# A four-layer image network on one core: small matmuls of the second layer and of the norms in quarters of the array, with a smaller unit time in the planner

## The chip, the core and the metric

The kernel runs on one core of a Trainium2 chip. The core has five engines that work side by side, each through its own queue in order: TensorE (PE; its weight loads are listed as PEld), VectorE (DVE), ScalarE (ACT), GpSimd (POOL) and SyncE (SP), which here only issues transfers. ACT and POOL issue transfers too. Instructions of different engines wait for each other by semaphores. The metric is the device time of one execution in microseconds (us), as the median of several runs.

## What is computed

The input x is 4 images of 96 channels and 64 x 64 pixels in f32. Four layers follow, cut here to their shape:

```python
x = x + ss2d(group_norm(x))               # layer 0: layer norm, projection, 3x3 depthwise conv,
                                          #   four selective scans of 192 channels x 16 states
                                          #   over 4096 pixels, layer norm, gate, projection
x = x + deform_conv(group_norm(x))        # layer 1: offsets = conv3x3(x, 27 outputs), then
                                          #   9 taps sampled at these offsets (bilinear), conv
t = tokens(x)
t = t + fourier(ln(t)); t = t + ffn(ln(t))      # layer 2: 96 -> 192, FFT along 4096 tokens and back
t = t + linear_attention(ln(t)); t = t + ffn(ln(t))   # layer 3
```

The offsets' convolution of layer 1 has 27 outputs for each pixel: 9 vertical offsets, 9 horizontal ones and 9 mask values. A layer norm (`ln`) subtracts the mean over the 96 channels of a pixel and divides by the root of the variance.

## The kernel before

The work of an image is cut into 8 chunks of 512 pixels (`CH`), and channels lie on the partitions. The selective scans of layer 0 are cut into 1536 *units*: 4 images x 4 directions x 4 stretches of 1024 pixels x 3 groups x 8 units, and each has 8 channels x 16 states on the 128 partitions. A unit takes: a transfer of the decay exponents (L874), an exponential on ACT (L895, `da`), two matmuls on PE that spread the inflow over the partitions (L901, `db`, two buffers), a product on DVE (L915), the recurrence itself on DVE (L918, `hh`), two instructions on POOL (L925, L927), and a share of the sums over the states on PE (L946, `py`). The sums already use quarters of PE's columns: each matmul writes 32 partitions of one PSUM tile (`py[p0 : p0 + 32]`) with 32 weight columns. L941 adds an earlier direction's result in four such quarters.

All other work is written as Python generators that are laid between the units. Stream `ends` holds layer 0 before the scan for each image and then layers 2 and 3 of each image; stream `middle` holds layer 0 behind the scan and layer 1. An image's later layers can start only when its scans are done, so the last image's stand behind the last unit.

The order of instructions is fixed when the program is built, by a planner. Each step of a generator names its costs in us by engine (`cost(pe=2.6)`), and class `Clock` adds them up by engine. After every unit `unit()` raises `due` by `PACE`. A step is placed if the engines that it uses have room: the planned end of each may be at most a few us (`AHEAD`) after the present, and the step's `ready`, which its earlier steps set, may not lie after the end of its first engine. `pipe()` runs several chains of such steps at once; a chain may take and give back counted tokens (`takes`, `frees`), for instance for a buffer. The chip knows nothing of this clock: it sees one order for each engine and the semaphores.

The functions that the change touches:

- `centred()` (L447) is the first half of a layer norm, called 4 times each for layer 0, the Fourier layer, attention and the two feed-forward layers, 20 in all. For each chunk PE multiplies by a centring matrix (L457, `lnc`), ACT writes the squares (L462 or L465, `lnq`) and copies the centred values. Then PE sums the squares of chunk j over the channels into row j of a tile of 128 rows (L468, `lnv`, with 128 weight columns of which one is not zero). `inv_sqrt_steps()` makes the root's inverse of the whole tile on ACT and DVE, and `spread()` (L483, `lnb`) brings row j back onto all partitions.
- `offsets()` (L1113) is layer 1 up to the offsets. `chunk(j)` adds nine taps into one tile (L1149, `po`, 96 weight columns of which 27 are not zero), ACT adds the bias (L1159, `oc`), PE transposes the pixels (L1165, `pt`) and the offsets (L1170, `pm`), ACT copies both, and SP writes the pixels into a table in DRAM in eight transfers (L1178, `table<-pix`). The nine taps come in three steps of three.
- `behind()` (L968) has a layer norm over 192 channels, with the sums at L1022 (`va`) and two chunks in rows 0 and 1.

```python
nc.tensor.matmul(var, lhsT=self.to_row[C][:C, 7 - j : 135 - j], rhs=sq, ...)   # L468
```

Of the kernel before, what the change touches and what calls it, by code (L numbers as in the profile page):

```python
# [8 lines left out]
F32 = mybir.dt.float32  # L9
# [16 lines left out]
CH = 512  # L26
# [18 lines left out]
def prepare(x, **w):  # L45
# [65 lines left out]
    om = np.concatenate([ow[0::2], ow[1::2], w["L1_conv_mask_w"].reshape(9, C, 9)])  # L111
    a["wom"] = wide(om.transpose(1, 2, 0), 96)
    ob = w["L1_conv_offset_b"]
# [85 lines left out]

PACE = 4.8  # L200

# [59 lines left out]
def pipe(net, chains, width, every=0, **tiles):  # L261
# [5 lines left out]
    while True:  # L267
# [9 lines left out]
        for n, chain in enumerate(active):  # L277
            if chain.new and not net.has_bank():
                continue
            if any(a.done <= chain.done + every for a in active[:n]):  # L280
                continue
            if not all(free[tag] for tag in chain.takes):
                continue
            if clock.has_room(known.get((chain.kind, chain.done), (1.0,) * 4), chain.ready):
                break
        else:
            yield BLOCKED
            continue
# [44 lines left out]
class Net:  # L333
# [3 lines left out]
    def __init__(self, ctx, tc, ins):  # L337
# [4 lines left out]
        self.psum = ctx.enter_context(tc.tile_pool(name="mm", bufs=3, space=PSUM))  # L342
        for name in ("vecs", "ident", "cen96", "grp3"):
            setattr(self, name, self.load(name, self.const))

        self.to_row = {}
        for n in (C, DI):
            t = self.to_row[n] = self.const.tile([128, 135], F32, name=f"to_row{n}")
            nc.vector.memset(t, 0.0)
            nc.vector.memset(t[:, 7:8], 1.0 / n)  # L350
        self.eps = self.const.tile([128, 1], F32, name="eps")
# [95 lines left out]
    def centred(self, x, cen, dst, key, pool, bias=None):  # L447
# [3 lines left out]
        var = self.mm(f"lnv{key}")  # L451
        self.hold(1)

        def chain(j):
            cs = slice(j * CH, (j + 1) * CH)
            pc = self.mm(f"lnc{key}_{j}")
            nc.tensor.matmul(pc, lhsT=cen, rhs=x[:, cs], start=True, stop=True)  # L457
            pc = pc[:C]
            sq = pool.tile([C, CH], F32, name=f"lnq{key}_{j}", tag="lnq", bufs=2)
            d, view = dst(j)  # L460
            if bias is None:
                nc.scalar.activation(sq, pc, AF.Square)  # L462
                nc.scalar.copy(d, view(pc))
            else:
                nc.scalar.activation(sq, pc, AF.Square, bias=bias)  # L465
                nc.scalar.activation(d, view(pc), AF.Identity, bias=bias)
            yield cost(pe=1.1, act=1.2)
            nc.tensor.matmul(  # L468
                var, lhsT=self.to_row[C][:C, 7 - j : 135 - j], rhs=sq, start=(j == 0), stop=(j == NCH - 1)
            )  # L470
            yield cost(pe=1.0)

        yield from pipe(self, (chain(j) for j in range(NCH)), 2)
        self.rstd = pool.tile([128, CH], F32, name=f"lns{key}", tag="lns", bufs=1)
# [35 lines left out]
class Layer0:  # L510
# [95 lines left out]
    def normed_rows(self, b, x, pad, rows, as_rows):  # L606
# [3 lines left out]
        with tc.tile_pool(name=f"l0n{b}", bufs=2) as sm:  # L610
# [21 lines left out]
            def chain(j):  # L632
                pb = net.spread(rs, j, C, f"0_{b}")
                yield cost(pe=1.2, holds=1)
# [333 lines left out]
    def behind(self, b):  # L968
# [6 lines left out]
        with (  # L975
# [4 lines left out]
            for j0 in range(NCH - HB, -1, -HB):  # L980
# [18 lines left out]
                def centred(i):  # L999
# [12 lines left out]
                    for g, (o, c0, n) in enumerate(((ca, 0, 128), (cc, 128, D2))):  # L1012
# [9 lines left out]
                        nc.tensor.matmul(  # L1022
                            var,
                            lhsT=net.to_row[DI][:n, 7 - i : 135 - i],
                            rhs=sq,
                            start=(i == 0 and g == 0),
                            stop=(i == HB - 1 and g == 1),
                        )
# [8 lines left out]
                def gated(i):  # L1037
# [5 lines left out]
                    nc.sync.dma_start(zc, self.z_d[b][128:, cs])  # L1043
                    pb = net.spread(rstd, i, 128, key)
                    yield cost(pe=1.2, holds=1)
# [25 lines left out]
class Layer1:  # L1071
# [41 lines left out]
    def offsets(self, b, om):  # L1113
# [3 lines left out]
        with tc.tile_pool(name=f"l1a{b}", bufs=1, side="right") as pre:  # L1117
# [26 lines left out]
            def chunk(j):  # L1144
                r0 = j * NR
                po = net.mm(f"po{b}_{j}", 96)
                for k in range(9):
                    dy, dx = divmod(k, 3)
                    nc.tensor.matmul(  # L1149
                        po,  # L1150
                        lhsT=wom[:, k, :],
                        rhs=pad[:, r0 + dy : r0 + dy + NR, dx : dx + W],
                        start=(k == 0),
                        stop=(k == 8),
                    )
                    if k in (2, 5):
                        yield cost(pe=2.6, holds=1, takes="oc" if k == 5 else "")
                oc = pre.tile([27, CH], F32, name=f"oc{b}_{j}", tag="oc")
                nc.scalar.activation(oc, po[:27], AF.Identity, bias=net.vec(V_OMB, 27))  # L1159
                yield cost(pe=2.6, act=0.7, new=True, takes="pix")  # L1160

# [7 lines left out]
                for q in range(4):  # L1169
                    nc.tensor.transpose(pm[:, q, :], oc[:, 128 * q : 128 * q + 128], net.ident[:27, :27])  # L1170
                nc.scalar.copy(om[:, 4 * j : 4 * j + 4, :], pm)
# [292 lines left out]
def normed(net, t, tl, key, pool):  # L1464
# [6 lines left out]
    def chain(j):  # L1471
        cs = slice(j * CH, (j + 1) * CH)
        pb = net.spread(rs, j, C, key)
        yield cost(pe=1.2, holds=1)
        net.nc.vector.tensor_mul(tl[:C, cs], tl[:C, cs], pb)  # L1475
        yield cost(dve=0.7)
# [248 lines left out]
```

## Time and profile before

| | us |
|---|---|
| median of 5 runs | 9117.53 (9101.12 to 9141.04) |
| profiled execution | 9100.43 |
| its span, first to last instruction | 9098.3 |
| first and last start of a scan recurrence (L918) | 369.6 and 7983.1 |
| busy PE, DVE, POOL, ACT | 6723.8 (74%), 6975.9 (77%), 6367.4 (70%), 4183.9 (46%) |
| mean granted clock of TensorE | 0.822 |
| L1149, the taps: busy, 576 records | 266.3 |
| L468, the sums of squares: busy, 320 records | 173.2 |

The page of a profile lists for each line its busy time, the mean of one instruction in ns, the idle time of its engine just before it and what ended that idle time. The chain of waits goes back from the last instruction, at each step to what released it. A matmul of f32 data stands as two records. The trace is of one execution; the profiled one lies a little below the lowest of the five timed ones.

### The profile page before, as it was taken

What the parts mean: (1) busy time and instruction counts of PE and PEld (TensorE: products, weight loads), DVE (VectorE), ACT (ScalarE), POOL (GpSimd) and SP (SyncE); (2) the same over time, 40 slices, a digit from 0 to 9 for tenths busy, and PEclk for the clock granted to TensorE, in tenths of its full rate; (3) what the DMA queues carried; (4) which work ended last, traced back from release to release, by engine and by line L of the source; (5) the groups of instructions that cost most, each with busy time, mean ns of one, the idle gap of its engine ahead of it and who ended that gap; (6) DMA issues with size and microseconds to landing.
All of it is one profiled execution on the core that took longest, in us unless ns stands there. A gap on an engine that the chain in (4) does not pass through costs nothing.

```text
span 9098.3 us, 93017 instructions
## 1 busy us (share of the span) xinstructions
PE 6723.8 (74%) x31832; PEld 3064.7 (34%) x31832; DVE 6975.9 (77%) x4932; ACT 4183.9 (46%) x5798; POOL 6367.4 (70%) x4755
## 2 busy tenths in 40 slices
PE   6565966697766679776778877788777768885487
PEld 2111311132222234211245642244543425433273
DVE  0367877887898888878898989889899988836614
ACT  3564667565554435555533335533344344431123
POOL 0476678766889998787799977766799966627701
PEclk8676978798878789788889888788888878886698
DMA  1466777777877887787788786677777777824410
GB/s 50 126 181 173 184 193 215 199 186 175 211 209 211 214 210 207 199 212 199 206 208 228 208 196 173 170 190 186 210 200 198 197 165 192 196 57 138 133 58 12
DMA packets 775821, 1609.05 MB, mean 177 GB/s; under 512 B 247665, under 2 KB 338829, under 8 KB 773238
## 3 DMA queue, kind: packets, MB, share of 16 engines
q10 hardware_dynamic: 244224, 843.17, 36.9%
q1 hardware_dynamic: 457398, 533.38, 21.8%
q0 software_dynamic: 73728, 226.57, 9.4%
q8 instruction: 253, 4.15, 0.2%
q14 instruction: 218, 1.79, 0.1%
HBM read 1346.50 MB, written 256.29 MB: 176 GB/s over the span
## 4 chain that ended last, share of the span: by engine, by line
PE 32%; DVE 21%; POOL 16%; DMA 14%; issue 9%; ACT 5%; SPq 1%; ACTq 0%; DVEq 0%; POOLq 0%
DVE hh L918 9%; POOL hh L927 7%; DVE db L915 5%; POOL g L1251 5%; PE pc L662 4%; PE py L946 4%; PE f L1371 3%; PE db L901 3%; PE ps L1277 2%; PE po L1149 2%; DMA du<-du 2%; DVE g L1260 2%; PE pd L1293 2%; DMA g<-table,idx 2%; DMA da<-de 1%
## 5 line engine op out<-in xcount | busy, mean ns | idle before, releaser
L927 POOL TENSOR_TENSOR hh<-hh,bc 128x1024 f32<-128x1024 f32 x1536 | 3670.5, 2391 | 350.4 <-DVE hh L918 233.7
L918 DVE TENSOR_TENSOR_SCAN hh<-da,st,db 128x1024 f32<-128x1024 f32 x1152 | 2703.7, 2347 | 220.0 <-PE py L946 71.1
L915 DVE TENSOR_TENSOR db<-db,bc 128x1024 f32<-128x1024 f32 x1536 | 1869.2, 1217 | 409.2 <-PE db L901 399.2
L895 ACT ACTIVATE da<-da,w_al 128x1024 f32<-128x1024 f32 x1536 | 1743.3, 1148 | 729.9 <-DMA da<-de 278.1
L901 PE MATMUL db<-du,rep 96*128 96x512 bf16 x3072 | 1062.2, 433 | 820.6 <-DVE hh L918 756.1
L1251 POOL DMA_INDIRECT g<-table,idx x1152 | 1339.6, 1163 | 400.4 <-issue 227.7
L946 PE MATMUL py<-hh,w_fold 128*32 128x512 f32 x6144 | 1082.6, 731 | 114.0 <-POOL hh L927 90.6
L918 DVE TENSOR_TENSOR_SCAN hh<-da,db 128x1024 f32<-128x1024 f32 x384 | 878.2, 2287 | 61.3 <-PE py L946 9.4
L1277 PE MATMUL ps<-w_ident,g 128*96 128x128 f32 x3744 | 610.9, 323 | 377.1 <-issue 236.1
L901 PEld LDWEIGHTS <-rep 96*128 96x128 bf16 x3072 | 275.3, 104 | 1741.6 <-issue 1167.7
L1260 DVE TENSOR_TENSOR g<-g,wt 128x1152 f32<-128x1152 f32 x384 | 687.2, 1790 | 162.6 <-DMA g<-table,idx 159.9
L1285 ACT COPY st<-ps 96x384 f32<-96x384 f32 x384 | 182.4, 476 | 1249.3 <-PE ps L1277 1088.2
L925 POOL COPY st<-hh 128x1 f32<-128x1 f32 x1152 | 271.5, 236 | 657.7 <-DVE hh L918 623.4
L1277 PEld LDWEIGHTS ps<-w_ident,g 128*96 128x96 f32 x3744 | 499.1, 150 | 611.5 <-issue 354.8
L749 POOL TENSOR_TENSOR w<-w,ex 128x512 f32<-128x512 f32 x192 | 245.9, 1281 | 518.3 <-ACT w L746 512.5
L662 PE MATMUL pc<-pad,wc 96*128 96x512 f32 x1152 | 540.9, 617 | 45.1 <-DMA wc<-wc_d 41.5
L752 DVE SCALAR_TENSOR_TENSOR rl<-pd,lw 128x512 f32<-128x512 f32 x192 | 130.9, 682 | 473.9 <-POOL lw L750 463.3
L771 PE MATMUL pr<-ex,w_ident 128*128 128x512 f32 x384 | 290.1, 847 | 151.6 <-POOL ex L761 75.2
L946 PEld LDWEIGHTS py<-hh,w_fold 128*32 128x32 f32 x6144 | 161.2, 120 | 634.2 <-issue 386.7
L1517 POOL CAST xqf<-fl 96x512 fp8e5<-96x512 f32 x64 | 45.3, 715 | 438.1 <-DVE fl L1475 390.9
L662 PEld LDWEIGHTS pc<-pad,wc 96*128 96x128 f32 x1152 | 222.5, 198 | 329.6 <-issue 314.1
L1293 PE MATMUL pd<-st,wdc 96*128 96x256 f32 x1152 | 311.5, 422 | 1.0 <-ACT zt L688 0.8
(249 smaller groups left out, 9485.3 us busy)
## 6 DMA issues: line engine op xcount, KB each, us to landing
da<-de ACTq DMA_DIRECT2D x1536, 512.0 KB
du<-du SPq DMA_DIRECT2D x512, 192.0 KB
bc<-bcd SPq DMA_DIRECT2D x128, 512.0 KB
du<-du SPq DMA_DIRECT2D x128, 384.0 KB
y<-yb SPq DMA_DIRECT2D x384, 128.0 KB
de<-rl SPq DMA_DIRECT2D x128, 256.0 KB
m<-in_dft SPq DMA_DIRECT2D x128, 256.0 KB
ad<-y ACTq DMA_DIRECT2D x192, 128.0 KB
```

The costliest lines, as they stand in the source:

```text
L662: nc.tensor.matmul(pp, lhsT=wc[:, q, g * 128 : (g + 1) * 128], rhs=pad[:, r0 + dy : r0 + dy + NR, dx : dx + W], start=(q == 0), stop=(q == 8),
L771: nc.tensor.matmul(pr, lhsT=net.ident, rhs=ex, start=True, stop=False)
L895: self.net.nc.scalar.activation(u.da, u.da, AF.Exp, scale=self.al[:, a : a + 1])
L901: self.net.nc.tensor.matmul(db[:, h, :], lhsT=self.rep[:96, u.s % 4, :], rhs=u.du[u.s // 4][:, h * CH : (h + 1) * CH], start=True, stop=True,)
L915: nc.vector.tensor_mul(u.db, u.db, u.bc[:, 0, :])
L918: nc.vector.tensor_tensor_scan(u.along(u.hh), u.along(u.da), u.along(u.db), first, ALU.mult, ALU.add)
L927: self.net.nc.gpsimd.tensor_mul(u.hh, u.hh, u.bc[:, 1, :])
L946: nc.tensor.matmul(py[p0 : p0 + 32], lhsT=self.fold[:, u.i, :], rhs=hc[:, h * CH : (h + 1) * CH], start=u.sums["add"] is None and u.i == 0 ...
L1251: nc.gpsimd.indirect_dma_start(out=g[:, k, :], out_offset=None, in_=self.tables[b % 2], in_offset=bass.IndirectOffsetOnAxis(ap=idx[:, n : ...
L1260: nc.vector.tensor_mul(g4, g4, w4.unsqueeze(2).to_broadcast([128, 12, C]))
L1277: nc.tensor.matmul(pt[:, k, :], lhsT=g[:, k, c * C : (c + 1) * C], rhs=net.ident, is_transpose=True, start=(c == 0), stop=(c == corners - 1),)
L1293: nc.tensor.matmul(po, lhsT=wdc[:, k, :], rhs=st[:, k, :], start=(k == 0), stop=(k == 8))
```

## The change

There are three parts. First, the offsets' convolution uses 32 weight columns instead of 96, and tap k writes partitions 32 (k mod 4) to 32 (k mod 4) + 31 of `po`, so four taps use four quarters of the array's columns. The four partial sums come out on 128 partitions, and the matmul that turned the offsets now multiplies by a constant matrix `add4`, which adds the four parts while it transposes. The nine taps are one step of the planner, and the activation is a step of its own. Second, `centred()` keeps four squares and sums them together into four quarters of `var`, so that chunk j's variance stands in row 32 (j mod 4) + j // 4; `spread()` reads these rows, and the buffers of squares become four. The sums are chains of their own, which take a token that each of the four chunks gives back when it is placed. In `behind()` the two chunks' sums go to the two halves of the tile. Third, `PACE` is 4.7 instead of 4.8.

```diff
-    a["wom"] = wide(om.transpose(1, 2, 0), 96)
+    a["wom"] = wide(om.transpose(1, 2, 0), 32)
+    a["add4"] = (np.arange(128)[:, None] % 32 == np.arange(27)[None]).astype(f)
...
-PACE = 4.8
+PACE = 4.7
...
-            if not all(free[tag] for tag in chain.takes):
+            if not all(free[tag] > 0 for tag in chain.takes):
...
         def chain(j):
+            yield wait(new=True, takes="sq")
...
-            sq = pool.tile([C, CH], F32, name=f"lnq{key}_{j}", tag="lnq", bufs=2)
+            sq = sqs[j] = pool.tile([C, CH], F32, name=f"lnq{key}_{j}", tag="lnq", bufs=4)
...
-            yield cost(pe=1.1, act=1.2)
-            nc.tensor.matmul(
-                var, lhsT=self.to_row[C][:C, 7 - j : 135 - j], rhs=sq, start=(j == 0), stop=(j == NCH - 1)
-            )
-            yield cost(pe=1.0)
-
-        yield from pipe(self, (chain(j) for j in range(NCH)), 2)
+            yield cost(pe=1.1, act=1.2, frees=f"v{j // 4}")
+
+        def sums(r):
+
+            yield wait(takes=f"v{r}")
+            for q in range(4):
+                nc.tensor.matmul(
+                    var[32 * q : 32 * q + 32],
+                    lhsT=self.to_row[C][:C, 1 - r : 33 - r],
+                    rhs=sqs[4 * r + q],
+                    start=(r == 0),
+                    stop=(r == 1),
+                )
+            yield cost(pe=1.3, frees="sq sq sq sq")
+
+        def chains():
+            for r in range(2):
+                for q in range(4):
+                    yield chain(4 * r + q)
+                yield sums(r)
+
+        yield from pipe(self, chains(), 5, every=-99, sq=4, v0=-3, v1=-3)
...
-                pb = net.spread(rs, j, C, f"0_{b}")
+                pb = net.spread(rs, 32 * (j % 4) + j // 4, C, f"0_{b}")
...
-                            var,
-                            lhsT=net.to_row[DI][:n, 7 - i : 135 - i],
+                            var[64 * i : 64 * i + 64],
+                            lhsT=net.to_row[DI][:n, 1:65],
...
-                po = net.mm(f"po{b}_{j}", 96)
+                po = net.mm(f"po{b}_{j}")
+
                 for k in range(9):
                     dy, dx = divmod(k, 3)
+                    p0 = 32 * (k % 4)
                     nc.tensor.matmul(
-                        po,
+                        po[p0 : p0 + 32],
...
-                        start=(k == 0),
-                        stop=(k == 8),
+                        start=(k < 4),
+                        stop=(k >= 5),
                     )
-                    if k in (2, 5):
-                        yield cost(pe=2.6, holds=1, takes="oc" if k == 5 else "")
-                oc = pre.tile([27, CH], F32, name=f"oc{b}_{j}", tag="oc")
-                nc.scalar.activation(oc, po[:27], AF.Identity, bias=net.vec(V_OMB, 27))
-                yield cost(pe=2.6, act=0.7, new=True, takes="pix")
+                yield cost(pe=3.0, holds=1, takes="oc")
+                oc = pre.tile([128, CH], F32, name=f"oc{b}_{j}", tag="oc")
+                nc.scalar.activation(oc, po, AF.Identity, bias=net.vec(V_OMB))
+                yield cost(act=0.7, new=True, takes="pix")
...
-                    nc.tensor.transpose(pm[:, q, :], oc[:, 128 * q : 128 * q + 128], net.ident[:27, :27])
+                    nc.tensor.matmul(
+                        pm[:, q, :], lhsT=oc[:, 128 * q : 128 * q + 128], rhs=net.add4, start=True, stop=True
+                    )
```

More of the change, by code (lines that the diff above doesn't have):

```diff
@@ L342, in __init__ @@
         self.psum = ctx.enter_context(tc.tile_pool(name="mm", bufs=3, space=PSUM))
-        for name in ("vecs", "ident", "cen96", "grp3"):
+        for name in ("vecs", "ident", "cen96", "grp3", "add4"):
             setattr(self, name, self.load(name, self.const))
@@ L347, in __init__ @@
         for n in (C, DI):
-            t = self.to_row[n] = self.const.tile([128, 135], F32, name=f"to_row{n}")
+            t = self.to_row[n] = self.const.tile([128, 65], F32, name=f"to_row{n}")
             nc.vector.memset(t, 0.0)
-            nc.vector.memset(t[:, 7:8], 1.0 / n)
+            nc.vector.memset(t[:, 1:2], 1.0 / n)
         self.eps = self.const.tile([128, 1], F32, name="eps")
@@ L452, in centred @@
         self.hold(1)
+        sqs = {}
         def chain(j):
+            yield wait(new=True, takes="sq")
             cs = slice(j * CH, (j + 1) * CH)
@@ L1022, in centred @@
                         nc.tensor.matmul(
-                            var,
-                            lhsT=net.to_row[DI][:n, 7 - i : 135 - i],
+                            var[64 * i : 64 * i + 64],
+                            lhsT=net.to_row[DI][:n, 1:65],
                             rhs=sq,
-                            start=(i == 0 and g == 0),
-                            stop=(i == HB - 1 and g == 1),
+                            start=(g == 0),
+                            stop=(g == 1),
                         )
@@ L1043, in gated @@
                     nc.sync.dma_start(zc, self.z_d[b][128:, cs])
-                    pb = net.spread(rstd, i, 128, key)
+                    pb = net.spread(rstd, 64 * i, 128, key)
                     yield cost(pe=1.2, holds=1)
@@ L1472, in chain @@
         cs = slice(j * CH, (j + 1) * CH)
-        pb = net.spread(rs, j, C, key)
+        pb = net.spread(rs, 32 * (j % 4) + j // 4, C, key)
         yield cost(pe=1.2, holds=1)
```

## The prediction

> **What bounds the kernel now.** I read first the stretches: before the first scan step (0 to 370 us), the scan (to 7983), the last image's convolution layer (to 8642), the rest alone. Columns: PE, PEld, DVE, ACT, POOL.
>
> ```profile
> 0.00:370.00 370.00, 225.77 (x452) 87.74 (x453) 26.31 (x53) 163.84 (x203) 39.13 (x38) 0.79 0.23 65
> 370.00:7983.00 7613.00, 5724.26 (x27128) 2490.89 (x27127) 6470.43 (x4227) 3736.13 (x5026) 5887.73 (x4341) 0.83 0.76 196
> 7983.00:8642.00 659.00, 399.25 (x1225) 219.91 (x1224) 350.31 (x468) 145.33 (x301) 401.41 (x344) 0.71 0.41 111
> 8642.00:9098.00 456.00, 374.47 (x3028) 266.11 (x3028) 128.85 (x185) 138.61 (x270) 39.10 (x33) 0.90 0.12 35
> ```
>
> In the scan DVE is busy 85%, POOL 77%, PE 75%: no engine fills it, and 1143 us of DVE idle time is what better order or less work elsewhere can win. Next who waited for whom there:
>
> ```profile
> DVE db L915 <- PE db L901: 377.5, 186, 26.6
> DVE rl L752 <- POOL lw L750: 191.7, 86, 13.8
> DVE hh L918 <- PE py L946: 80.5, 66, 9.9
> ...
> PE pr L775 <- ACT du L773: 116.3, 69, 8.1
> ```
>
> (us, times, longest.) A late PE costs DVE 458 us, the largest part. Then the rows of the matmuls concerned, in the scan: the offsets' convolution, the quarter-column matmuls that exist already, the variances:
>
> ```profile
> L1149 PE MATMUL po<-pad,w_wom 96*96 96x512 f32 x432 | 202.7, 607 | 3.9 <-DVE d L1420 2.9 <-ACT pix L1167 0.9
> L941 PE MATMUL py<-ad,w_ident 128*32 128x512 f32 x768 | 131.0, 762 | 43.8 <-ACT yb L957 43.8
> L468 PE MATMUL lnv<-lnq,to_row 96*128 96x512 f32 x128 | 67.4, 630 | 0.5 <-ACT lnq L462 0.5
> L468 PE MATMUL lnvf<-lnqf,to_row 96*128 96x512 f32 x68 | 36.4, 643 | 0.0
> ```
>
> A f32 matmul is two records here. The timeline shows what a quarter costs (start, length):
>
> ```profile
> 3174.11 1.06 PE L941 MATMUL py<-ad,w_ident 128*32 128x512 f32 x8
> 3174.99 0.61 PE L946 MATMUL py<-hh,w_fold 128*32 128x512 f32 x4
> ```
>
> Four quarter matmuls of 512 columns hold PE 0.88 us, until the next group starts: the price of one whole matmul (0.86). L946's groups of four, whose moving data are four different tiles' halves, start as close.
>
> **The offsets' convolution.** The chain of waits in the last image's:
>
> ```profile
> 8107.99 7.90 PE po L1149 x18
> 8115.89 0.33 PE pt L1165 x4
> 8116.22 0.36 PE pm L1170 x4
> 8116.58 7.90 PE po L1149 x18
> ...
> 8166.70 0.44 SPq L1178
> 8167.18 0.62 SPq L1178
> ```
>
> Nine taps take 7.7 us (18 x 0.429, the distance of two records); in three rounds of quarters (4, 4, 1) 3 x 0.88 = 2.64. A chunk saves 5.1 us of PE. The activation keeps its 512 columns (678 ns), and the four products that replace transposes also have 27 moving columns, so I take 0.36 us for them again.
>
> *Last image, nothing beside it:* a chunk came every 8.58 us. PE would need 2.64 + 0.33 + 0.36 + gaps, about 3.6. Late next is SP: eight table writes a chunk, 0.62 to 0.65 us each, 5.2 us. Eight chunks save 7 x (8.58 - 5.2) = 24 us; 35 if SP kept pace with PE, 14 if the writes landed slowly (DMA is busy 0.49 of 67 us there, 33 us' worth in what would be 42). I take 24.
>
> *Three images beside the scan:* 24 chunks x 5.1 = 122 us of PE. The chain of waits holds L1149 for 15.9% of 2420 to 2720 us, 14.6% of 4350 to 4570 and 21.0% of 6240 to 6470: 128 of the 203 us busy. Two thirds of that is 84 at most; none if DVE's own work takes its place. DVE is at 85%, so I take 60.
>
> **The variances.** A norm has eight products with L468, 6.9 us; after, two rounds, 1.76: 5.1 us less PE. But the order changes: before, each product followed its own square with another in between; now PE takes four products directly behind the fourth centring product, and stands until ACT has squared it. In the chunks' pipe the sums are released when the fourth chunk is *queued*, not when the planner has ACT finished, so this wait is unseen by the planner. Behind it on PE's queue are db and py of the next units, for which DVE waits. The built order shows it: in the scan mostly "db, lnc, lnv x4", on ACT with one or two decay exponentials (1.15 us) in between.
>
> *In the scan* there are 12 norms (196 records of 16). The chain holds L468 there for 33 us; three quarters, 24, is the gain at most. The cost: 24 waits; the nearest row is PE's wait for ACT at L775, 116.3 / 69 = 1.7 us each, so 40 us, of which the second db buffer hides half. I take a gain of 5 (bounds +24 and -50).
>
> *Alone:* image 3's four norms run 17.5, 17.5, 20.9 and 14.2 us from first to last matmul (timeline). After, ACT sets it: two activations of 0.59 + 0.57 a chunk, eight of them 9.3, a start of 1.2, a break of about 1.4 where the second four follow the first sums, and the last sums: 13. Saved 70 - 52 = 18; none if the break is twice as long and the matmuls after idle time stay slow (at 8651.32 the first four records took 3.75 us, later four take 1.72), 25 at best. Between 7983 and 8100 two norms stand in a PE-dense chain: 10. The first norm (at 37 us) is not on the chain, which runs there through SP's clearing of the tables: 0. The added load of the small matrix lies in that SP queue: 1 us.
>
> [...]
>
> **The smaller unit time.** 1536 units x 0.1 is 154 us of the planner's time. But nothing on the chip waits for that clock; it only sets how the instructions are interleaved. The scan's rows show that the chip has its own pace:
>
> ```profile
> 900.00:1300.00 400.00, 208.93 (x91) 0.87 0.70 186
> ...
> 4950.00:5190.00 240.00, 93.89 (x40) 0.89 0.82 212
> 5400.00:5800.00 400.00, 221.52 (x95) 0.80 0.68 167
> ```
>
> That is 4.4, 6.0 and 4.2 us a unit, under one constant of 4.8. And the built order of both kernels is nearly one: the other work lies on average from 8 units earlier (feed-forward) to 3 later (convolution) of 1536, and behind the last py there are 2561 PE instructions against 2570. The same work stands beside each unit as before. So I take 0, with bounds of -154 (real units follow the planner's) and +30 (the row "rl <- POOL lw", 192 us, grows by a sixth as units come closer).
>
> **Sum.** 60 + 5 in the scan, 24 + 18 + 10 behind it, -1 at the start: 116 us. The profiled execution took 9100.4 us (span 9098.3 and 2.1 around it), 17 below the median of the five runs, 9117.5, and below the lowest of them. 9100 - 116 = 8984; I name 8990, as a median lies a little higher.
>
> **Rivals.** *The units follow the clock.* DVE has 15% idle, and 154 us of it would close if the planner's tighter interleave is also the chip's. For it: stretches at 4.8 us with every engine under 83%. Against: equal order. 8984 - 154 = 8830 in full; the stretches of gathers, about a quarter of the scan, where a unit takes 5.3 to 6.0 us of work, can't give theirs, so 8984 - 115 = about 8870. *The PE time saved in the scan is covered.* DVE and POOL take over the chain; only what lies behind the scan counts: 9100 - 51 = 9049. For it: POOL at 77% and DMA at 0.76. Against: 128 us of chain. *Slower: the sums' wait.* PE stands in 24 places before the sums with the next units' db behind it. Without these waits the sum is 116 + 20 = 136, so each must cost DVE 5.7 us before it is gone, more than a unit; at the longest wait of the L775 row, 8.1 us, they cost 194, which gives 9100 - 136 + 194 = 9158. Against: the mean there is 1.7. *It doesn't do what it says:* quarters run one after another; then nothing is saved and about 9120 results. L941 excludes it almost.
>
> **Chances.** Forecast (8930 to 9035) 0.51; clock followed 0.20; covered 0.20; waits 0.05; quarters in turn 0.04. The range, 8865 to 9070, leaves out the last two and the ends of the first rivals. 0.3% (27 us of 9117.5) is about what a measurement of this kernel can tell from no change: under 9090 is faster, 0.87; within, 0.07 (the quarters' case and an end of the covered one); slower 0.06.
>
> **What would show it.** L1149 at about 260 - 170 = 90 us busy in all; chunk distance in the last image near 5.2 us with SP in the chain; a new wait of PE L468 on ACT, 1 to 3 us each; the scan ending near 7983 - 65 = 7918; what follows it 1115 - 52 = 1063 long. A scan shorter by 150 proves the clock's case; one as long as before the covered one. DVE waiting for db by over 450 us would prove the waits'.

## The result and the profile after

The changed kernel takes 9150.97 us (median of 32 runs, 9098.48 to 9174.29), the kernel before 9118.63 (58 runs beside it): a ratio of 1.0033, 95% interval 1.0024 to 1.0042. Forecast was 8990; the change costs some 30 us where 128 were to be saved.

The profiled execution of the changed kernel took 9172.25 us, near the top of its own runs, so its trace shows a loss of 72 us against the profile of before, where the medians show 32. Its stretches, divided at the same events as before (first scan step, end of the scan, end of the last image's convolution layer; columns: span, then busy time of PE, PEld, DVE, ACT, POOL, then the granted clock, DMA share, GB/s):

```profile
0.00:372.00 372.00, 222.12 (x452) 84.89 (x453) 25.25 (x52) 163.18 (x203) 39.19 (x38) 0.79 0.22 65
372.00:8075.00 7703.00, 5676.77 (x27278) 2433.52 (x27279) 6500.55 (x4239) 3736.24 (x5039) 5909.37 (x4342) 0.81 0.76 194
8075.00:8725.00 650.00, 351.42 (x1214) 194.89 (x1209) 332.77 (x449) 143.17 (x299) 373.27 (x343) 0.67 0.42 115
8725.00:9170.00 445.00, 375.04 (x3023) 266.16 (x3022) 128.84 (x185) 134.73 (x267) 39.14 (x33) 0.86 0.11 33
```

The start is 3 us later, the two stretches behind the scan are 20 us shorter together where 52 were forecast, and the scan is 90 us longer between these bounds (86 from the first recurrence to the end of the last, 7616 to 7702). PE is busy 47 us less in it: the matmuls were saved, and time was lost all the same. DVE does 30 us more there, of which 18 are work that no longer lies behind the scan (479 to 462 us), and the other 60 are DVE's idle time. Who ended it, in the scan (us, times, longest):

```profile
DVE db L934 <- PE db L920: 424.0, 173, 25.4
DVE rl L771 <- POOL lw L769: 181.0, 75, 15.3
DVE g L1282 <- DMA g<-table,idx: 79.6, 29, 6.5
DVE hh L937 <- PE py L965: 78.2, 74, 5.5
DVE hh L937 <- ACT da L914: 35.1, 14, 9.5
```

Two rows of before that the prediction does not show:

```profile
DVE g L1260 <- DMA g<-table,idx: 69.1, 38, 6.3
DVE hh L918 <- ACT da L895: 7.5, 6, 3.2
```

The row of `db` holds one wait of 25.4 us before the first recurrence, which the row of before (377.5), taken from 370 us on, leaves out. Without it DVE waited 398.6 us for `db`, 21 more than before, though PE has less to do. The waits for the exponentials on ACT grew by 28 us and those for gathers by 10: no single row holds the 60 us. The matmuls in question, in the scan (records | busy us, mean ns | idle before and what ended it):

```profile
L960 PE MATMUL py<-ad,w_ident 128*32 128x512 f32 x768 | 134.3, 780 | 34.1 <-ACT yb L976 34.1
L1170 PE MATMUL po<-pad,w_wom 96*32 96x512 f32 x432 | 74.1, 661 | 17.3 <-ACT pix L1187 11.1 <-DVE rl L771 4.2 <-ACT du L797 2.0
L477 PE MATMUL lnv<-lnq,to_row 96*32 96x512 f32 x128 | 28.8, 604 | 4.0 <-ACT lnq L469 3.5 <-ACT lnq L466 0.4
L477 PE MATMUL lnvf<-lnqf,to_row 96*32 96x512 f32 x80 | 16.3, 607 | 0.6 <-ACT lnqf L466 0.6
```

The convolution's row fell from 202.7 to 74.1 us, the variances' from 103.8 (67.4 + 36.4) to 45.1. PE waited 4.6 us in all for the squares: the wait that the planner doesn't see is nearly nothing. In the last image's convolution the chain of waits reads (start, length):

```profile
8176.52 5.28 PE po L1170 x36
8182.46 0.85 PE pm L1190 x8
8185.00 0.63 SPq L1200
...
8224.84 0.62 SPq L1200
```

Nine taps take 5.28 / 2 = 2.64 us in quarters, as forecast, and SP's table writes are the next limit. The first writes of two chunks lie 5.3 to 6.5 us apart, 5.6 in the mean; forecast was 5.2, from the length of a write (0.62 to 0.65 us), where the distance of two is 0.66. From the first tap to the last table write it is 50.7 us instead of 74.3, 24 less, as forecast. But what follows that write takes 943 us instead of 927, although the four norms in it are 17 us shorter. Which instruction loses these 33 us isn't isolated.

### The profile page after: what moved, and what is told of

Same layout as the page of the kernel before. It is cut to its first block, busy times and chain, and to the rows that moved or that the text cites. A ratio compares the mean times of both kernels' runs of the same rounds, so it can differ in the third digit from the quotient of the medians.

```text
span 9170.5 us, 93180 instructions
## 1 busy us (share of the span) xinstructions
PE 6625.4 (72%) x31960; PEld 2979.5 (32%) x31960; DVE 6987.4 (76%) x4923; ACT 4177.3 (46%) x5807; POOL 6361.0 (69%) x4755
## 4 chain that ended last, share of the span: by engine, by line
PE 28%; DVE 20%; POOL 17%; DMA 16%; issue 10%; ACT 5%; SPq 2%; ACTq 1%; another core or an unknown queue 1%; DVEq 0%; POOLq 0%
DVE hh L937 9%; POOL hh L946 8%; DVE db L934 5%; POOL g L1273 5%; PE pc L681 4%; PE py L965 3%; DMA du<-du 3%; PE f L1393 3%; PE db L920 3%; PE ps L1299 2%; DMA da<-de 2%; DVE g L1282 2%; PE pd L1315 2%; DMA m<-in_dft 1%; DMA g<-table,idx 1%
## 5 line engine op out<-in xcount | busy, mean ns | idle before, releaser
L914 ACT ACTIVATE da<-da,w_al 128x1024 f32<-128x1024 f32 x1536 | 1740.8, 1147 | 750.0 <-DMA da<-de 266.2
L920 PE MATMUL db<-du,rep 96*128 96x512 bf16 x3072 | 1087.7, 442 | 886.5 <-DVE hh L937 839.7
L965 PE MATMUL py<-hh,w_fold 128*32 128x512 f32 x6144 | 1114.2, 752 | 79.7 <-POOL hh L946 66.3
L1282 DVE TENSOR_TENSOR g<-g,wt 128x1152 f32<-128x1152 f32 x384 | 707.5, 1844 | 116.6 <-DMA g<-table,idx 114.9
L758 PE MATMUL pd<-xd,w_dtw 103*64 103x512 f32 (+1 forms) x512 | 261.1, 775 | 82.4 <-DVE rl L771 38.7
```

The source lines that it names most:

```text
L914: self.net.nc.scalar.activation(u.da, u.da, AF.Exp, scale=self.al[:, a : a + 1])
L920: self.net.nc.tensor.matmul(db[:, h, :], lhsT=self.rep[:96, u.s % 4, :], rhs=u.du[u.s // 4][:, h * CH : (h + 1) * CH], start=True, stop=True,)
L965: nc.tensor.matmul(py[p0 : p0 + 32], lhsT=self.fold[:, u.i, :], rhs=hc[:, h * CH : (h + 1) * CH], start=u.sums["add"] is None and u.i == 0 ...
L1282: nc.vector.tensor_mul(g4, g4, w4.unsqueeze(2).to_broadcast([128, 12, C]))
```

## The experiments

Ratios are to the kernel before in runs on the same chip. "Scan" goes from the first recurrence to the end of the last, "behind" from there to the end, both in one profiled execution, which lies up to 33 us off the median (conv_told_62).

| kernel | median us | ratio, 95% interval | scan | behind |
|---|---|---|---|---|
| before | 9118.63 | | 7616 | 1113 |
| after | 9150.97 | 1.0033 (1.0024 to 1.0042) | 7702 | 1096 |
| pace_only | 9133.4 | 1.0017 (1.0002 to 1.0031) | 7566 | 1181 |
| after_pace48 | 9190.94 | 1.0080 (1.0057 to 1.0103) | 7717 | 1094 |
| var_only | 9090.17 | 0.9980 (0.9962 to 0.9997) | 7623 | 1079 |
| conv_only | 9162.16 | 1.0051 (1.0033 to 1.0068) | 7718 | 1089 |
| conv_old_plan | 9084.95 | 0.9972 (0.9959 to 0.9984) | 7637 | 1085 |
| conv_late28 | 9235.68 | 1.0143 (1.0124 to 1.0163) | 7668 | 1187 |
| conv_pix3 | 9171.48 | 1.0062 (1.0043 to 1.0081) | 7722 | 1083 |
| conv_three_steps10 | 9197.98 | 1.0083 (1.0064 to 1.0102) | 7764 | 1089 |
| conv_told_46 | 9124.98 | 1.0013 (1.0001 to 1.0024) | 7660 | 1099 |
| conv_told_62 | 9116.05 | 1.0006 (0.9995 to 1.0018) | 7620 | 1092 |
| conv_one_step78 | 9116.26 | 0.9996 (0.9983 to 1.0009) | 7628 | 1119 |
| conv_told_94 | 9124.73 | 1.0019 (1.0005 to 1.0033) | 7629 | 1124 |
| before_told_27 | 9146.17 | 1.0035 (1.0020 to 1.0050) | 7674 | 1107 |
| before_told_25 | 9146.55 | 1.0026 (1.0014 to 1.0039) | 7649 | 1128 |
| after_old_steps | 9107.74 | 0.9997 (0.9985 to 1.0009) | 7595 | 1147 |
| old_steps_48 | 9056.42 | 0.9929 (0.9910 to 0.9947) | 7615 | 1070 |
| old_steps_49 | 9193.18 | 1.0081 (1.0060 to 1.0102) | 7716 | 1105 |
| all_told_27 | 9116.25 | 1.0000 (0.9983 to 1.0018) | 7651 | 1091 |

### Which part costs

**pace_only** is the kernel before with the smaller unit time; **after_pace48** is the changed kernel with the old one.

```diff
-PACE = 4.8
+PACE = 4.7
```

> The kernel before with the unit time 4.7 alone. Theory P (the smaller unit time lays more work ahead of the units than the engines hold, and costs what the rest gains): slower by 40 to 80 us. Theory W (PE stands before the new sums of squares, with the next units' inflow behind it): no change, within 25 us. Theory S (the offsets' chunks come faster, and their table writes crowd the queue that also loads the units' data): no change, within 25 us. Theory K (TensorE with less work is granted a lower clock, and its other matmuls give the time back): no change, granted clock 0.82.

> The changed kernel with the unit time back at 4.8. Theory P: faster than the kernel before by 50 to 100 us. Theories W, S and K: as the changed kernel, 10 to 50 us slower than before.

Alone the smaller unit time costs 16 us, in the changed kernel it gains some 43 (1.0080 to 1.0033). So it isn't what makes the change slow, and theory P fails in both runs. It also isn't nothing on the chip. The scan and what lies behind it, in pace_only:

```profile
366.00:7932.00 7566.00, 5642.42 (x25867) 2389.14 (x25887) 6490.71 (x4203) 3705.60 (x4973) 5901.68 (x4341) 0.82 0.77 197
7932.00:9113.00 1181.00, 876.82 (x5500) 578.51 (x5494) 505.51 (x679) 312.56 (x623) 437.26 (x376) 0.81 0.29 81
```

The scan is 50 us shorter and the end 68 us longer: PE has 1,261 records fewer in the scan than before (27128) and 1,247 more behind it (4253 before, both stretches). Work that finds no room in shorter units is left for the end.

**var_only** is the kernel before with the variances in quarters, **conv_only** with the convolution in quarters, both with the old unit time; the edits are those hunks of the change.

> The kernel before with the variances in quarters alone, unit time 4.8. Theory W: slower by 30 to 80 us, with a wait of PE or its weight loads for ACT at the sums of squares of 1 to 3 us each. Theory S: faster by 20 to 40 us. Theory K: within 25 us, granted clock near 0.815. Theory P: faster by 20 to 40 us.

> The kernel before with the offsets' convolution in quarters alone, unit time 4.8. Theory W: faster by 50 to 100 us. Theory S: slower by 20 to 50 us, lost in the stretches of the three offsets' convolutions beside the scan. Theory K: within 25 us, granted clock near 0.81, and the rows of the spread (db) and of the sums over the states (py) some per cent longer. Theory P: faster by 30 to 80 us.

The variances gain 0.2%, so theory W fails: PE standing before the sums is not what costs. The convolution alone loses more than the whole change. In conv_only the scan grows by 102 us with the sums of busy time within 21 us of before on PE and 8 on the others, and DVE's idle time grows by 105. DVE's waits in conv_only's scan:

```profile
DVE db L917 <- PE db L903: 427.7, 182, 26.6
DVE rl L754 <- POOL lw L752: 201.1, 94, 14.1
DVE g L1265 <- DMA g<-table,idx: 106.2, 46, 7.2
DVE pos L1207 <- DMA y<-yb: 50.0, 3, 18.5
```

`db` came later by 50 us in sum (377.5 before), gathers by 37 (69.1), the base positions by 18 (31.9) and `rl` by 9 (191.7).

### Is it the hardware or the order?

**conv_old_plan** has conv_only's instructions, but the planner is told three steps of 2.6 us as before, so that PE's order is that of the kernel before, instruction by instruction.

```diff
-                yield cost(pe=3.0, holds=1, takes="oc")
+                    if k in (2, 5):
+                        yield cost(pe=2.6, holds=1, takes="oc" if k == 5 else "")
...
-                yield cost(act=0.7, new=True, takes="pix")
+                yield cost(pe=2.6, act=0.7, new=True, takes="pix")
```

> The offsets' convolution in quarters, but told to the planner as before (three steps of 2.6 us): PE's order of instructions is that of the kernel before, one for one. Theory S (what costs is that the cheap chunks are placed twice as close, 8 in 13 units in place of 26, so that their table writes crowd SP, the DMA engines and ACT's buffers): faster than before by 10 to 50 us, the last image's stage 24 us shorter, the scan as long or shorter. Theory K (less PE work, lower granted clock, slower matmuls): slower by 20 to 50 us, clock 0.805 as in the convolution alone. Theory O (any new order shifts the time by some tens of us, without a cause in the writes): faster by about 24 us, the last stage alone, since the order is old.

With the old order the same quarters make the kernel faster by 0.28%, 25 us; what lies behind the scan is 28 us shorter in its profile. So the quarters don't cost time, the new order does. And the PE time saved in the scan was worth nothing that these runs show: its scan is no shorter. The three stretches in which the convolution lies (units 420 to 456, 806 to 840, 1186 to 1222) show why. First before, then conv_old_plan:

```profile
2432.00:2602.00 170.00, 144.56 (x485) 47.70 (x484) 145.43 (x96) 92.00 (x132) 123.52 (x96) 0.87 0.80 213
4364.00:4533.00 169.00, 137.75 (x459) 45.76 (x458) 139.34 (x92) 87.54 (x127) 118.68 (x92) 0.86 0.78 200
6259.00:6407.00 148.00, 133.54 (x860) 65.20 (x859) 133.56 (x89) 59.38 (x77) 94.11 (x73) 0.97 0.77 201
```

```profile
2435.00:2600.00 165.00, 125.25 (x511) 38.93 (x513) 144.73 (x96) 91.65 (x130) 123.53 (x98) 0.76 0.83 217
4377.00:4540.00 163.00, 120.35 (x488) 34.63 (x486) 138.73 (x92) 88.40 (x126) 120.50 (x94) 0.74 0.81 211
6278.00:6421.00 143.00, 122.12 (x889) 56.49 (x887) 133.53 (x89) 60.94 (x77) 94.93 (x73) 0.79 0.81 209
```

DVE was busy 145 of 170 us, 139 of 169 and 134 of 148 before, as much as PE. With PE relieved, 5, 6 and 5 us are gained, 16 in all, and DVE is then busy 85 to 93%. More was hardly to be had: before, DVE waited for PE only 6.7, 10.5 and 0.5 us in these stretches, 18 in all, and 7.5 in conv_old_plan. Its longest wait in each was one for the base positions, which a DMA loads (12.9, 10.2 and 8.8 us). The first stretch of before (DVE's waits):

```profile
DVE pos L1202 <- DMA w_base<-in_base: 12.9, 1, 12.9
DVE db L915 <- PE db L901: 6.7, 8, 1.9
```

In the rest of the scan, which has the same instructions in the same order, 37 us are lost in this one profile. It lies 7 us above its median and that of before 18 below its own, so part of the 37 may belong to the two executions; the medians leave 25 us of gain, which is what lies behind the scan.

PE's own busy time fell by 48 us in these stretches, where the convolution's row alone fell by 104 (187.3 to 83.2). Of the 56 between, 19 are the products that replace the transposes: 64 records a stretch instead of 32, 29.7 us instead of 10.6. The rest goes with a lower granted clock: 0.87 to 0.76, 0.86 to 0.74, 0.97 to 0.79. Rows that the change doesn't touch got longer, here in the first stretch, before and then in conv_old_plan:

```profile
L1149 PE MATMUL po<-pad,w_wom 96*96 96x512 f32 x138 | 63.1, 596 | 0.0
L901 PE MATMUL db<-du,rep 96*128 96x512 bf16 x72 | 24.3, 421 | 5.7 <-DVE hh L918 5.7
L946 PE MATMUL py<-hh,w_fold 128*32 128x512 f32 x144 | 22.3, 695 | 1.4 <-issue 1.4
```

```profile
L903 PE MATMUL db<-du,rep 96*128 96x512 bf16 x72 | 26.0, 448 | 19.5 <-DVE hh L920 19.4
L1153 PE MATMUL po<-pad,w_wom 96*32 96x512 f32 x138 | 25.0, 630 | 0.7 <-issue 0.7
L948 PE MATMUL py<-hh,w_fold 128*32 128x512 f32 x144 | 24.4, 756 | 2.4 <-ACT yb L959 2.3
```

`db` takes 448 ns instead of 421, `py` 756 instead of 695, and before `db` PE now waits 19.4 us for DVE instead of 5.7. In this stretch less matmul work (PE busy 125 of 165 us instead of 145 of 170) went with a lower mean clock for what is left, 0.76 instead of 0.87.

The same units in conv_only, which has the same instructions in its own order, show where that order loses:

```profile
2435.00:2639.00 204.00, 134.95 (x560) 43.27 (x559) 151.36 (x100) 103.00 (x150) 142.55 (x111) 0.74 0.78 203
4410.00:4614.00 204.00, 143.38 (x700) 60.83 (x703) 153.19 (x113) 78.13 (x114) 138.00 (x107) 0.79 0.77 193
6327.00:6511.00 184.00, 141.56 (x902) 64.64 (x901) 145.50 (x98) 80.22 (x113) 98.75 (x84) 0.81 0.71 179
```

They take 592 us instead of 487, as much more as the whole scan. DVE does 32 us more work there, and it waits for PE for 72 us instead of 18. In the changed kernel they take 553 us, 66 of the 86 that its scan loses, and DVE waits 51 for PE. A longer stretch alone is no loss, since work can move into it: in conv_told_62 below they take 537 us, and the rest of its scan 45 less than before.

### Two suspects beside the planner

**conv_late28** spreads the convolution's chunks again, in conv_only's form: the pixel buffer is given back 28 us of planned time later. **conv_pix3** has three pixel buffers where conv_only has two; the planner's count of them is raised likewise, and its order stays the same.

```diff
+                yield wait(28.0)
                 yield wait(frees="pix")
```

```diff
-                pix = pre.tile([128, 4, C], F32, name=f"pix{b}_{j}", tag="pix", bufs=2)
+                pix = pre.tile([128, 4, C], F32, name=f"pix{b}_{j}", tag="pix", bufs=3)
```

> The offsets' convolution in quarters with its true cost (one step of 3.0 us), but a chunk's write token comes back 28 us of planned time later, so that the chunks are spread over 24 units again. Theory S: faster than before by 0 to 45 us; faster than the convolution alone by 45 to 90 us. Theory K: slower than before by 20 to 50 us. Theory O: anywhere within 50 us of before.

> The offsets' convolution in quarters as in the change (chunks close together, the same order), with three buffers for the pixels in place of two, so that ACT waits less for a table write to land. Theory S with ACT's buffer as the choke: 20 to 50 us faster than the convolution alone, within 25 us of before. Theory S with SP and the DMA engines as the choke: as the convolution alone, 30 to 60 us slower than before. Theory K: as the convolution alone. Theory O: as the convolution alone.

Around the first image's convolution (units 384 to 576) spread chunks lose as much, 54 us, as close ones (58 in conv_only). conv_told_62 and conv_one_step78 below lose 6 and nothing there, with chunks over 17 units against 13. So crowded table writes are not the main cause at that place. Around the second one (768 to 960) spread chunks gain 20 us where close ones lose 70, so crowding is not excluded everywhere. conv_late28 as a whole is slower than any theory had it. Its end is 74 us longer than before, 27 of them in the last image's convolution, which the planned delay also holds. A third buffer changes nothing, and its stretches of 96 units agree with conv_only's within 7 us: the same order gives the same time, place by place.

### The price that the planner is told

These five have conv_only's instructions and differ in the price of the convolution in the plan: three steps of 1.0, or one of 4.6, 6.2, 7.8 or 9.4 us (conv_only: one of 3.0).

```diff
-                yield cost(pe=3.0, holds=1, takes="oc")
+                yield cost(pe=7.8, holds=1, takes="oc")
```

> The convolution in quarters alone, in three steps as before, each told to the planner at 1.0 us, its true cost. Theory D: slower than before by 25 to 70 us, as the convolution in the change alone, lost around the chunks (units 384 to 480, 768 to 960) in waits of DVE for the inflow (db) and for gathers. Theory G: faster than before by 0 to 40 us.

> The convolution in quarters alone, its nine taps one step as in the change, but told to the planner at the old 7.8 us. Theory D (what costs is the planned PE time that the cheap chunk frees: the planner fills it with other work, and PE then stands in front of that with the next units' inflow behind it): within 25 us of before or faster, except that the order leaves 223 PE instructions more behind the scan, which may add up to 30 us there. Theory G (what costs is the block of nine taps that no inflow can pass): slower than before by 30 to 70 us, as the convolution in the change alone.

> The kernel before with the convolution in quarters, its one step told to the planner at 4.6 us (the same step at 3.0 gave 1.0051, at 7.8 0.9996). Theory D (each us of PE time that the planner is told to be free is filled with other work that the engines can't follow): between the two, 1.002 to 1.005, and the loss in DVE's idle time in the scan. Theory O (any new order moves the time by tens of us either way, whatever the told price): anywhere from 0.996 to 1.013, no place between the neighbours.

> The same step told at 6.2 us. D: 1.000 to 1.003, below the step told at 4.6. O: anywhere from 0.996 to 1.013.

> The same step told at 9.4 us, more than the whole-array convolution took. D: 0.996 to 1.000, not above the step told at 7.8. O: anywhere from 0.996 to 1.013.

At a price of 3.0 in three steps or one the ratio is 1.0083 and 1.0051, then 1.0013, 1.0006, 0.9996, and 1.0019 at 9.4. Three steps at the low price are no better than one, and one step of 7.8 is no worse than before, so the grain of the steps (theory G) is not the cause. The low prices are the dear ones, as theory D has it: a chunk whose price is lower leaves planned PE time, the planner lays more work of other streams into it, and PE is at that work before it comes to the next units' `db`. DVE's wait for `db` in the scan fits: 510 us in conv_three_steps10, 428 in conv_only, 387 to 401 at the four prices from 4.6 on, 394 in conv_old_plan. But D had more at 4.6 (1.002 to 1.005), and it said that 9.4 is not above 7.8, which it is by 0.0023, with intervals that just meet. From 4.6 on there is no trend.

### The order alone

**before_told_27** and **before_told_25** are the kernel before; only the planner's price of each of the three convolution steps is 0.1 us higher or lower.

```diff
-                        yield cost(pe=2.6, holds=1, takes="oc" if k == 5 else "")
+                        yield cost(pe=2.7, holds=1, takes="oc" if k == 5 else "")
...
-                yield cost(pe=2.6, act=0.7, new=True, takes="pix")
+                yield cost(pe=2.7, act=0.7, new=True, takes="pix")
```

> The kernel before, nothing changed but the planner's price of the three convolution steps, 2.7 instead of 2.6 us each, 0.3 us a chunk. D: within 0.002 of 1. O: a new order alone, 16664 lines of PE's order differ (names of tiles included), so 10 to 60 us either way.

> The kernel before, the planner's price of the three convolution steps 2.5 instead of 2.6 us. With 2.7 it took 1.0035 of the time. Theory O (any new order moves the time either way, no rule): anywhere from 0.993 to 1.010, as likely off by 10 us as not. A rule by the price (a low one costs, a high one gains) would give over 1.000 here, though it already failed at 2.7.

Both cost about as much as the whole change: 0.35% and 0.26%, 32 and 24 us, in opposite directions of the price, with not one instruction added or removed. The scan of before_told_27 and its waits:

```profile
369.00:8043.00 7674.00, 5730.94 (x27128) 2482.79 (x27141) 6483.68 (x4229) 3737.02 (x5030) 5895.49 (x4341) 0.82 0.76 195
```

```profile
DVE db L915 <- PE db L901: 427.1, 202, 25.1
DVE rl L752 <- POOL lw L750: 200.3, 86, 14.6
DVE g L1260 <- DMA g<-table,idx: 97.5, 32, 8.9
```

Every engine is busy as before to 14 us; the scan is 58 us longer, 47 of it DVE's idle time, and DVE's wait for `db` grew from 377.5 to 427.1 and the one for gathers from 69 to 98: the same signs as in conv_only, with the convolution as it was. Theory D, within 0.002, fails here; theory O, which had 10 to 60 us either way, holds. Both neighbours cost, and so does pace_only, 16 us: the order of the kernel before is better than these three. That any other order costs is not shown.

### All parts with another order

**after_old_steps** is the changed kernel with the planner told three steps of 2.6 as before; **old_steps_48** and **old_steps_49** are the same with a unit time of 4.8 and 4.9; **all_told_27** is old_steps_48 with three steps of 2.7.

> The changed kernel, all three parts, with the offsets' convolution told to the planner as three steps of 2.6 us. Theory S: faster than before by 20 to 70 us (the last stage 24, the variances 18, and what PE's freed time gives). Theory K: slower by 10 to 50 us. Theory O: anywhere within 50 us of before.

> All hardware parts of the change, the convolution told to the planner as before (three steps of 2.6), unit time 4.8. If the parts add (convolution with the old plan -23, variances -18): faster than before by 25 to 60 us. Theory O (any new order shifts the time by tens of us): anywhere within 40 us.

> As old_steps_48 with the unit time 4.9. If a larger unit time moves work from behind the scan into it (2318 PE instructions behind the last unit against 2377) at no cost: faster than old_steps_48 by 5 to 30 us. If the scan is filled already: slower than old_steps_48 by 10 to 40 us, all of it in the scan.

> Both convolution and variances in quarters, unit time 4.8, the convolution's three steps told at 2.7 instead of 2.6 us (2.6 gave 0.9929). O: the order is new, so anywhere from 0.990 to 1.005: the mean of the orders, some 25 us above the one of before, less the 40 us that the two parts save behind the scan, would be 0.998. If 0.9929 is a property of the parts and not of the order: 0.991 to 0.995.

With its price alone put back, the changed kernel goes from 1.0033 to 0.9997 (after_old_steps), 33 us. old_steps_48 beats both kernels, 0.9929, 64 us under before. But 0.1 us more in a price (all_told_27) gives all of it back, and 0.1 us in the unit time gives 0.9997 or 1.0081. The last, old_steps_49, is 137 us slower than old_steps_48 at the old price, and neither of its expectations had that. Scan and end, of old_steps_48 and then of all_told_27:

```profile
370.00:7985.00 7615.00, 5661.29 (x27242) 2408.43 (x27242) 6461.07 (x4229) 3740.49 (x5032) 5889.30 (x4341) 0.81 0.77 196
7985.00:9055.00 1070.00, 730.05 (x4268) 469.06 (x4266) 476.93 (x653) 278.42 (x563) 433.10 (x376) 0.77 0.30 83
```

```profile
370.00:8021.00 7651.00, 5664.11 (x27260) 2427.13 (x27259) 6484.36 (x4229) 3743.25 (x5039) 5911.00 (x4341) 0.81 0.76 195
8021.00:9113.00 1092.00, 732.32 (x4248) 470.04 (x4248) 473.12 (x643) 279.51 (x566) 421.62 (x376) 0.76 0.29 82
```

PE's busy time is the same within 3 us; the scan differs by 36 us and the end by 22. So 0.9929 is not a property of the parts: it is the best of six orders of the same instructions, which reach from there to 1.0081 with a mean of 1.0020. Its scan is as long as before, and its gain is 43 us behind the scan, where all_told_27 gains 22.

## Why the prediction was wrong

By its own steps, forecast and measured:

| step | forecast | measured |
|---|---|---|
| three images' convolution, in the scan | -60 | 0: the gain of conv_old_plan, 25 us, is all behind the scan |
| variances, in the scan | -5 | about 0: var_only's scan +7 |
| last image's convolution | -24 | -24 from its first tap to its last table write; -28 behind the scan in conv_old_plan |
| norms behind the scan | -28 | -34 behind the scan in var_only, -18 by its median |
| all behind the scan | -52 | -17 in the change, -43 in old_steps_48, -22 in all_told_27 |
| products that add the four parts, a chunk in the scan | as the transposes, 0.36 us | 1.12 us in the change (26.9 for 24 chunks), the transposes 0.44 |
| load of the added matrix | +1 | not resolved: with it the first recurrence is 3.0 us later in the change, 0.4 later in var_only, 2.5 earlier in conv_old_plan |
| smaller unit time | 0 | +16 alone, some -43 within the change |
| a new order | 0 | +24 and +32 at unchanged instructions; some +74 in the change (estimate below) |

**Two steps failed.** The first is "the chain of waits holds L1149 for ... 128 of the 203 us busy ... DVE is at 85%, so I take 60". A share of the chain is what a row holds now, not what is won when it goes. The prediction's own reserve, "none if DVE's own work takes its place", was the case: in the very stretches of the convolution DVE was busy 418 of 487 us, and 16 us came back there. The busy share of 0.85 was read rightly, it is 0.86 there. What was not read is how long DVE waited for PE in them: 18 us in the profile of before, against the 60 taken. The lower granted clock (0.87, 0.86 and 0.97 became 0.76, 0.74 and 0.79) and the longer adding products (29.7 us instead of 10.6) took part of the saved PE time besides. This is the rival named "covered", at 9049; with the norms as before it would be 9077, and with the order kept 9085 was measured.

The second is the larger: "the built order of both kernels is nearly one ... so I take 0". The evidence was a mean shift, 3 units for the convolution. Means hid what changed: in the traces' order on PE, the taps of the first image's eight chunks stood over 27 units (421 to 448) and now stand over 13 (423 to 436), while their mean moved by 5, to earlier ones. And the step assumed that a small change of order has a small cost. before_told_27 and before_told_25 show 24 to 32 us for a price 0.1 us off, and at an equal unit time every order with the low price was slower than that with the old one.

How the 1.0033 comes about can be estimated from the runs: conv_old_plan gives -0.0028 and var_only -0.0020, so the order of the changed kernel costs 0.0033 + 0.0048 = 0.0081, some 74 us. The same difference for the other orders, each ratio less what its parts gave, divides by the price. With the low price (3.0 in one step or in three) it is 0.0079 (conv_only), 0.0111 (conv_three_steps10), 0.0128 (after_pace48) and 0.0171 (conv_late28). With a price of 4.6 or more it is 0.0017 to 0.0035 for the three of before, 0.0024 to 0.0047 for the four of the convolution, 0.0045 and 0.0048 for after_old_steps and all_told_27, -0.0023 for old_steps_48, and 0.0129 for old_steps_49. So about half of the 0.0081 goes with the low price (0.0036 when it alone is put back), and the rest is what most other orders cost too. That is an estimate: var_only has a new order itself, and old_steps_49 shows that an order can cost as much without the low price.

**What was right.** Four quarters cost as much as one whole matmul (0.88 us against 0.86; 2.64 us for nine taps, forecast 2.64). SP is next in the last image, at 5.6 us a chunk (forecast 5.2). The four norms alone take 53.5 us (14.4, 13.0, 14.6, 11.5), forecast 52. The wait of the sums for ACT, the slower rival at 9158, is 4.6 us in the scan instead of 40: that rival is false, though the sign was its. The products that add the four parts, 0.85 us instead of the 0.36 taken, lie beside SP's writes in the last image, where that stage got as much shorter as forecast. "DVE waiting for db by over 450 us would prove the waits'": 398.6 here, and it is 427.1 without the change (before_told_27), so this sign wouldn't have told the waits' case from an order's. The clock's rival, -154 or -115, is seen in part: pace_only's scan is 50 us shorter, and the end gives it back.

**What stays open.** Which resource a less favourable order meets first isn't isolated: `db`, gathers, the base positions, `rl` and the exponentials on ACT come later, in shares that differ from order to order; in old_steps_49 `db` does so by only 16 us (393.8) while the scan is 99 us longer. What is lost behind the last table write in the changed kernel isn't isolated either. Why the order of the kernel before is better than its neighbours was not found.

## What to carry to other kernels

When a planner fixes the order of every engine's instructions, a change of a price is a change of the whole order: price the hardware's part with the old order kept (conv_old_plan), and the order's part by neighbouring prices with the old instructions (before_told_27), before either is believed. A gain or a loss of a few tenths of a per cent in such a kernel says little about the part that was changed, and a mean shift of positions says little about how closely work is packed. Before a saving is taken from a row's share of the chain of waits, read what the next engine waits for that engine in the very stretch: here that was 18 us, where the chain held 128 us of the row, and 16 us came back.

## What the runs showed of the hardware

Less matmul work went with a lower granted TensorE clock: 0.822 over the kernel before, where PE is busy 6724 us (0.817 in the mean of its timed runs), 0.809 in conv_old_plan with the same order and 6664 us (0.810), 0.805 in the changed kernel with 6625 us, and 0.798 to 0.805 in all the runs with all parts; in the convolution's stretches 0.87, 0.86 and 0.97 became 0.76, 0.74 and 0.79, and untouched rows took 6% (`db`, 421 to 448 ns) and 9% (`py`, 695 to 756 ns) longer in the first of them. Over the whole scan, where the clock was 0.81 instead of 0.83, they took 2% longer (433 to 441 and 731 to 745 ns).

Four f32 matmuls of 96 x 512 into four quarters of the columns took 0.88 us (the changed kernel's taps at 8176.52 us: 5.28 us for six rounds), one of 96 columns 0.86 (the taps of before at 8107.99 us: two records, 0.429 us apart).

One order reproduces: conv_pix3 and conv_only, two kernels with the same order, agree within 7 us in every stretch of 96 units. Two orders of the same instructions differ by up to 151 us in the medians (conv_old_plan and conv_late28), and by 137 for 0.1 us of the unit time (old_steps_48 and old_steps_49).
